# Two queues and half-matrix loads at the head of a fused linear-ReLU-residual kernel

## The chip, the cores and the metric

The kernel runs on one core of a Trainium2 chip. The metric is the device time of one execution in microseconds (us); the median of several runs is compared. A profile is one further execution recorded by the hardware profiler; the stretch it shows, from the first to the last recorded instruction, is called the span.

## The reference

`x` is 4 x 1024 x 512 float32, `cond_512` 4 x 256, `W` 1536 x 512, `b` 512. The batch of 4 is called rows below.

```
hidden = concatenate([cond, cond], -1)                 # 4 x 512
x_mean = mean(x, axis=1, keepdims=True)
fused  = concatenate([x, x_mean, hidden], -1)          # the last two repeated along L
out    = x + relu(fused @ W + b)
```

So W has three parts of 512 rows. The first multiplies x and is the large product. The second multiplies the mean of a row, the third the condition; with b they give one vector for each row, which is added to all 1024 lines of it.

## The kernel before

**Tiles.** x is cut into 32 tiles of 128 lines (eight for each row). For a tile the product needs x turned, with the 512 features on the partitions: four pieces (j = 0 to 3) of 128 x 128. W's first part lies in SBUF as `w_x`, 128 partitions x 4 x 512: partition p holds rows 4p to 4p + 3, and j picks one of the four.

**Precision by splitting.** A float32 value v is split into hi, its value rounded to float32r, and lo = v - hi. A product of one j is three matmuls of 128x512: hi x w_hi, hi x w_lo, lo x w_hi. A tile takes 12 of them, accumulated in one PSUM bank (`po`). The splits of W are `w_hi` (ScalarE, L361) and `w_lo` (VectorE, L363), those of x `hi` (ScalarE, L417) and `lo` (VectorE or GpSimd, L433).

**Turning x.** The first units (tile 0; tile 1; tiles 2 and 3; tiles 4 and 5) are turned by TensorE with an identity matrix (L390), from tiles of x as loaded. All others are turned by VectorE (L392) from a second load of x, called `z`, in pieces of 512 bytes.

**The bias of a row.** Sums of x come from the splitting (L417's accumulator, or L426). `acc` adds the mean's and the condition's parts (L491, L494, L497), is split (`acc_hi`, `acc_lo`, L512 and L516), and a matmul with a matrix of 1/L sums it over the partitions and copies it to all of them (`pb`, L522).

**The end of a tile.** Bias added, ReLU, x added, stored, by VectorE, ScalarE, GpSimd and SP in shares that are written out in sets.

**What sets the order.** A planner, `Plan`, holds for each step its engine's cost, what it depends on and a due time, replays them on a model of the engines, tries 1500 variations of the due times, and keeps the best. Each engine then carries out its steps strictly in that order. What comes before the plan begins is told to it by hand: `plan.done[key]` is when a load of the head is taken to land, `plan.free["sp"]` when the load queue is taken to be free. Of the loads of the head, all are issued by SP, in the order of the table in the code:

```python
for key, at, load in (
    (("x", 0, 0), 4.5, lambda: load_x(0, 0, 1)),
    (("w", 0), 5.7, lambda: load_w(0)),
    ...
    (("x", 0, 1), 8.25, lambda: load_x(0, 1, 1)),
    ...
    (("x", 0, 2), 10.2, lambda: load_x(0, 2, 2)),
    (("x", 1, 0), 11.6, lambda: load_x(1, 0, 2)),
):
```

Behind them SP issues the first quarter of W's second part (`w_mean`), its third part (`w_cond`) and the z pieces. A load is issued when the load eight places before it has landed.

**The head of each engine.** VectorE clears a tile `warm`; TensorE multiplies it nine times (`N_WARM`, L236), turns tile 0, turns the condition (`fill`, L399), multiplies `warm` four times more (`N_FILL`, L403), and then begins with the products ("part" for tiles 0 and 1, one matmul at a time; "product" for later tiles). ScalarE loads its table (L231), issues the load of `cond` (`c_sb`, L240), and splits. `FIRST` is the time from which due times are counted.

Of the kernel before, what the change touches and what calls it, by code (L numbers as in the profile page):

```python
# [11 lines left out]
BF16 = mybir.dt.bfloat16  # L12
AF = mybir.ActivationFunctionType
# [140 lines left out]
def kernel(  # L154
# [22 lines left out]
    nc = tc.nc  # L177
    B, L, D = x.shape
    H = cond.shape[1]
    P = 128  # L180
# [6 lines left out]
    G = 4  # L187
    S_BUFS = 15
    O_BANKS = 5
    N_FIRST = 1  # L190
# [1 line left out]
    Z_BUFS = 3  # L192
    X_BUFS = 4
    O_BUFS = 12
    FIRST = 6.8
    NEVER = 1000.0
    TURN_PE = (0, 1, 2, 3)
    ALONE = 28
# [1 line left out]
    KEEP = (0, 1, 2, 3, 4, 8, 9, 10, 16, 17)  # L200
    LO_POOL = {(r, u, j) for r in (1, 2) for u in (0, 1) for j in (1, 3)} | {(0, 4, 3)}

    N_FILL = 4

    const = ctx.enter_context(tc.tile_pool(name="const", bufs=1))
    xpool = ctx.enter_context(tc.tile_pool(name="xpool", bufs=X_BUFS))
# [10 lines left out]
    plan = Plan(["pe", "dve", "act", "pool", "sp", "aq"])  # L217
    nc_of = {"pe": nc.tensor, "dve": nc.vector, "act": nc.scalar, "pool": nc.gpsimd}

    xv = x.rearrange("r (k p) d -> r p k d", p=P)  # L220
    ov = out.rearrange("r (k p) d -> r p k d", p=P)
    zv = x.rearrange("r (n t) (i d) -> r i t n d", t=Q, i=NQ)
    Wv = W.rearrange("(s p j) o -> s p j o", p=P, j=J)


    warm = const.tile([P, 512], BF16, name="warm")
    nc.vector.memset(warm, 0.0)
    ones = const.tile([P, 1], F32, name="ones")
    nc.vector.memset(ones, 1.0)
    table_warm = const.tile([P, 1], F32, name="table_warm")  # L230
# [6 lines left out]
            pw[:, KH * B :], lhsT=warm[:, :P], rhs=warm[:, KH * B :], start=True, stop=True  # L237
        )
    c_sb = const.tile([B, H], F32, name="c_sb")
    nc.scalar.dma_start(out=c_sb, in_=cond)  # L240
    b_sb = const.tile([P, D], F32, name="b_sb")
    nc.gpsimd.memset(b_sb, 0.0)
    mean32 = const.tile([P, P], F32, name="mean32")
# [21 lines left out]
    xs, zs = {}, {}  # L265
    w_x = xpool.tile([P, J, D], F32, tag="x", name="w_x")
    w_mean = const.tile([P, J, D], F32, name="w_mean")

    def load_x(g, i=0, n=G):
        r, k = divmod(g * G, NK)  # L270
        if not i:
            xs[g] = xpool.tile([P, G, D], F32, tag="x", name=f"x{g}")
        nc.sync.dma_start(out=xs[g][:, i : i + n], in_=xv[r, :, k + i : k + i + n, :])  # L273

    def x_tile(t):
        return xs[t // G][:, t % G, :]
# [4 lines left out]
    def load_z(eng, u, i):  # L281
        r, k0, n = units[u]
        if u not in zs:
            zs[u] = zpool.tile([P, G * NQ, P], F32, tag="z", name=f"z{u}")
        i = (0, 2, 1, 3)[i]
        eng.dma_start(  # L286
            out=zs[u][i * Q : (i + 1) * Q, : n * NQ],
            in_=zv[r, i, :, k0 * NQ : (k0 + n) * NQ, :],
        )

    SP = 0.72
    SPZ2 = 1.85
    SPZ = 1.3
    def load_w(j):
        nc.sync.dma_start(out=w_x[:, j, :], in_=Wv[0, :, j])  # L295

    for key, at, load in (
        (("x", 0, 0), 4.5, lambda: load_x(0, 0, 1)),
        (("w", 0), 5.7, lambda: load_w(0)),
        (("w", 1), 6.9, lambda: load_w(1)),  # L300
        (("w", 2), 7.6, lambda: load_w(2)),
        (("x", 0, 1), 8.25, lambda: load_x(0, 1, 1)),
        (("w", 3), 8.9, lambda: load_w(3)),
        (("x", 0, 2), 10.2, lambda: load_x(0, 2, 2)),
        (("x", 1, 0), 11.6, lambda: load_x(1, 0, 2)),
    ):
        load()
        plan.done[key] = (at - plan.HANDOVER, 0.0, "sp")
    w_cond = xpool.tile([P, 2, KH, D], F32, tag="x", name="w_cond")

    def load_cond():
        nc.sync.dma_start(  # L312
            out=w_cond, in_=W[2 * D : 3 * D].rearrange("(s h p) o -> p s h o", p=P, h=KH)
        )
# [3 lines left out]
    def load_mean(j, n):  # L318
        nc.sync.dma_start(out=w_mean[:, j : j + n, :], in_=Wv[1, :, j : j + n])

    load_mean(0, N_FIRST) if N_FIRST else None
    plan.free["sp"] = 9.4 + SP * N_FIRST
    plan.add("cond", {"sp": 4 * SP}, [], 13, lambda e: load_cond(), later=2.5)
    plan.add("w_mean", {"sp": (J - N_FIRST) * SP}, ["cond"], 14,
             lambda e: load_mean(N_FIRST, J - N_FIRST), later=2.5)
# [1 line left out]
    for n, u in enumerate(by_z):  # L327
        c0 = piece_of[u, 0]
        for i in range(NQ):
# [10 lines left out]
            elif n or i:  # L340
                deps.append(("z", u, i - 1) if i else ("z", by_z[n - 1], NQ - 1 if n > N_BOTH else NQ - 2))
            plan.add(("z", u, i), {"sp": SPZ * units[u][2] / G}, deps, NEVER,
                     lambda e, u=u, i=i: load_z(nc.sync, u, i), later=3.0)
    plan.add(("x", 1), {"sp": 2 * SP}, [], NEVER, lambda e: load_x(1, 2, 2), later=3.0)
    x_order = ["w", 0, 1, "cond"] + list(range(2, B * NK // G))
    for n, g in list(enumerate(x_order))[4:]:
        was = x_order[n - X_BUFS] if n >= X_BUFS else None
        deps = ([] if was is None else [("w_lo", j) for j in range(J)] if was == "w" else
                [("add_cond", k) for k in range(KH)] if was == "cond" else
                [("finished", was * G + i) for i in range(G)])  # L350
        if n > 4:
            deps.append(("x", x_order[n - 1]))
        plan.add(("x", g), {"sp": 4 * SP}, deps, NEVER,
                 lambda e, g=g: load_x(g), later=3.0)


    w_hi = const.tile([P, J, D], F32R, name="w_hi")
    w_lo = const.tile([P, J, D], F32R, name="w_lo")
    for j in range(J):
        plan.add(("w_hi", j), {"act": 0.62}, [("w", j)], NEVER,  # L360
                 lambda e, j=j: nc.scalar.activation(w_hi[:, j, :], w_x[:, j, :], AF.Copy))  # L361
        plan.add(("w_lo", j), {"dve": 0.69}, [("w_hi", j)], NEVER,
                 lambda e, j=j: nc_of[e].tensor_tensor(  # L363
                     w_lo[:, j, :], w_x[:, j, :], w_hi[:, j, :].bitcast(F32), ALU.subtract))
# [14 lines left out]
    def turn(c):  # L379
        u, js = pieces[c]  # L380
        n = units[u][2]
        if c in by_pool:
            v = xT[c] = small.tile([P, G * P], F32, tag="xT", name=f"xT{c}")
        else:
            v = xT[c] = ps_x.tile([P, G * P], F32, tag="x", name=f"xT{c}")
        if u in TURN_PE:
            for i in range(n):
                x_t = x_tile(last_tile[u] - n + 1 + i).rearrange("p (a j) -> p j a", j=J)
                for m, j in enumerate(js):
                    nc.tensor.transpose(v[:, (m * n + i) * P : (m * n + i + 1) * P], x_t[:, j], ident)  # L390
        else:
            nc.vector.transpose(  # L392
                v[:, : n * P].rearrange("p (n t) -> p n t", t=Q),
                zs[u].rearrange("p n (a j) -> p n j a", j=J)[:, : n * NQ, js[0], :],
            )

    def fill():
        for h in range(KH):
            nc.tensor.transpose(  # L399
                pw[:, h * B : (h + 1) * B], c_sb[:, h * P : (h + 1) * P], ident[:B, :B]  # L400
            )
        for _ in range(N_FILL):
            nc.tensor.matmul(  # L403
                pw[:, KH * B :], lhsT=warm[:, :P], rhs=warm[:, KH * B :], start=True, stop=True
            )

    plan.add(("b",), {"act": 0.25}, [("w_hi", J - 1)], FIRST + 4, lambda e: nc.scalar.dma_start(
        out=b_sb[0:1, :], in_=b.rearrange("(o d) -> o d", o=1)), later=3.0)
    plan.add(("fill",), {"pe": 0.22 * N_FILL + 0.2}, [("turn", 0)], 5.8, lambda e: fill())

    def split_hi(c):
        u, js = pieces[c]
# [24 lines left out]
    for c, (u, js) in enumerate(pieces):  # L437
        r, k0, n = units[u]
# [9 lines left out]
        if r == 1 and c == first_piece[1]:  # L448
            deps.append(("term", 0, KH + J - 1))
        w = n * len(js)  # L450
        plan.add(("turn", c), {"pe": 0.12 * w} if u in TURN_PE else {"dve": 0.14 + 0.24 * w}, deps,
                 FIRST + 1.3 * c - 1.0 if u in TURN_PE else NEVER,
                 lambda e, c=c: turn(c))
# [19 lines left out]
    def turn_cond():  # L473
        nc.vector.tensor_scalar(bL, b_sb, float(L), None, ALU.mult)
        nc.vector.tensor_scalar(
            cT, pw[:, : KH * B].rearrange("p (h b) -> p h b", h=KH), float(L), None, ALU.mult
        )

    def add_cond(eng, k):
        eng.tensor_tensor(wc[:, k], w_cond[:, 0, k], w_cond[:, 1, k], ALU.add)  # L480
# [48 lines left out]

    plan.add(("turn_cond",), {"dve": 0.3}, [("fill",), ("b",)], FIRST + 5, lambda e: turn_cond())  # L530
    for k in range(KH):
        plan.add(("add_cond", k), {"pool": 1.33}, ["cond"], NEVER,
                 lambda e, k=k: add_cond(nc_of[e], k))
    n_term = 0
    for r in range(B):
# [3 lines left out]
        for n in range(KH + J):  # L539
            if n < KH:  # L540
                deps = [("add_cond", n), ("turn_cond",)]
                if n_term >= 3:
                    deps.append(before[0])
                plan.add(("weigh", r, n), {"act": 0.72}, deps, NEVER,
                         lambda e, r=r, n=n: weigh(r, n))
                plan.add(("term", r, n), {"pool": 1.33}, done + [("weigh", r, n)], NEVER,
                         lambda e, r=r, n=n: add_term(r, n))
                before = (before if n_term else [])[-2:] + [("term", r, n)]
                n_term += 1
            else:  # L550
                deps = [("total", r), "w_mean"]
                if n == KH:
                    plan.add(("acc", r), {"act": 0.61 if r else 0.73},
                             done + [("bias", r - 1)] if r else deps, NEVER,
                             lambda e, r=r: begin_acc(r))
                    cond_done, done = done, [("acc", r)]
                    if not r:
                        continue
                plan.add(("term", r, n), {"dve": 0.76}, done + deps, NEVER,
                         lambda e, r=r, j=n - KH: mean_term(r, j))  # L560
            done = [("term", r, n)]
        if not r:
# [4 lines left out]
                 lambda e, r=r: acc_split_lo(r))  # L567
        plan.add(("bias_product", r), {"pe": 0.5}, [("acc_lo", r)], NEVER,
                 lambda e, r=r: bias_product(r))
        plan.add(("bias", r), {"act": 0.61}, [("bias_product", r)], NEVER,  # L570
                 lambda e, r=r: bias_copy(r))
# [64 lines left out]
    for t in range(NT):  # L636
        r, k = divmod(t, NK)
        u = unit_of[r, k]
        for h in (0, 1) if t == LAST else (None,):
            key = (t, h) if h else t  # L640
# [7 lines left out]
            for j in range(J):  # L648
                c = piece_of[u, j]
                if t < SINGLY:  # L650
                    for n in range(3):
                        deps = [("lo" if n == 2 else "hi", c), ("w_lo" if n == 1 else "w_hi", j)]
                        plan.add(("part", t, j, n), {"pe": 0.234}, deps, FIRST + 1.4 * j + 0.7 * t + 0.234 * (n + 1),
                                 lambda e, t=t, j=j, n=n: product(t, j, None, (n,)))
# [4 lines left out]
                else:  # L659
# [3 lines left out]
                plan.add(("product", key, j), {"pe": 0.7 if h is None else 0.36},  # L663
                         deps, FIRST + 2.8 * t + (0.7 if h is None else 0.36) * (j + 1) + 1.4 * (h or 0), lambda e, t=t, j=j, h=h: product(t, j, h))
        room = [("stored", t - O_BUFS)] if t >= O_BUFS else []
        if t:
            room.append(("freed", t - 1))
        due = min(FIRST + 2.8 * (t + 9), FIRST + 2.8 * NT - 8)
        if t >= ALONE:
            for h in (0, 1) if t == LAST else (None,):  # L670
                key = (t, h) if h else t
# [52 lines left out]
```

## Time and profile before

| | us |
|---|---|
| median of 3 runs (lowest to highest) | 107.19 (106.97 to 108.67) |
| profiled execution | 107.74 |
| its span | 106.0 |
| TensorE busy with matmuls | 101.3 |
| VectorE busy | 77.5 |
| GpSimd busy | 72.9 |
| ScalarE busy | 59.3 |
| one 128x512 product, issue to result | 0.40 |
| first product starts, from the span's start | 6.91 |
| one 256 KB load of W's first part, issue to landing (median of four) | 5.4 |

PE stands for TensorE's matmuls, PEld for its weight loads, DVE for VectorE, ACT for ScalarE, POOL for GpSimd, SP for SyncE; a q behind a name is the engine's queue, where it issues loads. In a line of the timeline there stand the start, the time taken, the engine, the line of the code, the operation, output<-input, how many, and in brackets how long the engine was idle before and what ended it. A line of the windows gives a stretch, its length, the busy time of PE, PEld, DVE, ACT and POOL with the number of instructions, the granted clock, the DMA engines' mean share and GB/s. Matmuls overlap, so a busy PE is not a PE at its peak.

### The profile page before, as it was taken

The page shows a single profiled execution, that of the slowest core. Times are in us where ns is not written, and L with a number is a line of the kernel's source. Part 1 is how long each engine was busy: PE and PEld are TensorE (multiplying, and loading weights), DVE is VectorE, ACT ScalarE, POOL GpSimd, SP SyncE. Part 2 cuts the span into 40 slices and gives each one's busy share as a digit, 9 for nine tenths or more (in the row PEclk, how much of TensorE's full clock was granted, in tenths as well). Part 3 has the DMA queues.
Part 4 walks back from the last instruction along what each step waited for, and adds up shares of the span by engine and source line. Part 5 has one row for each costly group of instructions (what it writes and reads, how often), then busy time and mean ns, then how long its engine had stood idle before and what let it go on. Part 6 is the DMA issues. An engine that isn't in the chain of part 4 may idle for free.

```text
span 106.0 us, 1470 instructions
## 1 busy us (share of the span) xinstructions
PE 101.3 (96%) x445; PEld 79.1 (75%) x445; DVE 77.5 (73%) x119; ACT 59.3 (56%) x138; POOL 72.9 (69%) x66
## 2 busy tenths in 40 slices
PE   5999999999998999999999999999999999999980
PEld 2456878878886787878888887887887887888870
DVE  1058743296589889999699999997999992097460
ACT  5075356799639967795378878222888340262000
POOL 6000004942796999999999899994999999149400
PEclk9999999999999999999999999999999999999999
DMA  3799999999999999999999999999996995504942
GB/s 71 196 361 398 370 216 209 215 164 205 220 181 189 202 202 237 202 275 262 256 252 343 360 316 197 301 395 394 404 387 212 356 367 220 200 0 162 382 174 74
DMA packets 24193, 26.83 MB, mean 253 GB/s; under 512 B 1269, under 2 KB 14841, under 8 KB 24186
## 3 DMA queue, kind: packets, MB, share of 16 engines
q1 hardware_dynamic: 24176, 26.74, 94.6%
q8 instruction: 3, 0.05, 0.2%
q14 instruction: 4, 0.03, 0.1%
q10 hardware_dynamic: 10, 0.01, 0.0%
HBM read 18.36 MB, written 8.39 MB: 252 GB/s over the span
## 4 chain that ended last, share of the span: by engine, by line
PE 66%; DMA 26%; DVE 3%; SPq 1%; issue 1%; DVEq 0%
PE po_None L596 61%; DMA z<-in_x_dram 20%; DMA w_x<-in_L_cond_W_dram 5%; PE po L596 3%; PE pb L522 2%; DVE xT L392 1%; DVE acc L494 1%; DVE acc_lo L516 1%; DVE o L627 0%; SPq L295 0%; SPq L312 0%; SPq L273 0%; SPq L286 0%; PE po L591 0%; DVEq L392 0%
## 5 line engine op out<-in xcount | busy, mean ns | idle before, releaser
L596 PE MATMUL po_None<-w_hi,hi 128*128 128x512 f32 x124 | 49.8, 402 | 0.0
L596 PE MATMUL po_None<-w_lo,hi 128*128 128x512 f32 x124 | 49.2, 397 | 0.1
L596 PE MATMUL po_None<-w_hi,lo 128*128 128x512 f32 x124 | 49.2, 398 | 0.0
L622 POOL TENSOR_TENSOR o<-o,x 128x512 f32<-128x512 f32 x28 | 35.5, 1301 | 4.2 <-ACT o L619 4.1
L392 DVE STREAM_TRANSPOSE xT<-z 128x512 f32<-128x512 f32 (+1 forms) x28 | 28.5, 1041 | 4.7 <-DMA z<-in_x_dram 3.6
L417 ACT ACTIVATE hi<-xT 128x512 fp32r<-128x512 f32 (+1 forms) x38 | 20.4, 537 | 16.8 <-DVE xT L392 8.5
L596 PEld LDWEIGHTS po_None<-w_hi,hi 128*128 128x128 f32 x124 | 23.4, 189 | 6.3 <-ACT w_hi L361 0.5
L596 PEld LDWEIGHTS po_None<-w_lo,hi 128*128 128x128 f32 x124 | 23.4, 189 | 5.6 <-DVE w_lo L363 0.4
L596 PEld LDWEIGHTS po_None<-w_hi,lo 128*128 128x128 f32 x124 | 23.3, 188 | 5.5
L433 DVE TENSOR_TENSOR lo<-xT,hi 128x512 fp32r<-128x512 f32 (+1 forms) x29 | 16.3, 576 | 8.2 <-ACT hi L417 8.2
L619 ACT ACTIVATE o<-o 128x512 f32<-128x512 f32 x28 | 16.7, 628 | 2.0 <-POOL o L614 1.0
L614 DVE TENSOR_TENSOR o<-po_None,bias 128x512 f32<-128x512 f32 x18 | 11.7, 676 | 6.6 <-issue 4.9
L614 POOL TENSOR_TENSOR o<-o,bias 128x512 f32<-128x512 f32 x10 | 12.9, 1306 | 1.4 <-issue 1.4
L433 POOL TENSOR_TENSOR lo<-xT,hi 128x512 fp32r<-128x512 f32 (+1 forms) x9 | 11.1, 1241 | 2.9 <-ACT hi L417 2.9
L480 POOL TENSOR_TENSOR wc<-w_cond 128x512 f32<-128x512 f32 x2 | 2.5, 1289 | 15.1 <-DMA w_cond<-in_L_cond_W_dram 15.1
L497 DVE SCALAR_TENSOR_TENSOR acc<-w_mean,tot,acc 128x512 f32<-128x512 f32 x15 | 11.3, 755 | 1.5 <-ACT acc L491 1.0
L528 ACT ACTIVATE bias<-pb 128x512 f32<-128x512 f32 x4 | 2.4, 598 | 10.1 <-PE pb L522 10.1
L417 ACT ACTIVATION_READ_ACCUMULATOR hi<-xT 128x1 f32 x36 | 7.0, 194 | 0.0
L508 POOL TENSOR_TENSOR cond<-bL,term 128x512 f32<-128x512 f32 x4 | 5.2, 1297 | 1.8 <-ACT term L503 1.8
L503 ACT ACTIVATE term<-wc,cT 128x512 f32<-128x512 f32 x8 | 5.7, 720 | 1.2 <-POOL cond L508 0.8
L609 ACT ACTIVATE o<-po_None 128x512 f32<-128x512 f32 x10 | 5.7, 590 | 0.8 <-PE po_None L596 0.7
L390 PEld LDWEIGHTS xT<-ident,x 128*128 128x128 f32 x24 | 4.2, 206 | 1.7 <-issue 0.8
(51 smaller groups left out, 58.9 us busy)
## 6 DMA issues: line engine op xcount, KB each, us to landing
out_dram<-o SPq DMA_DIRECT2D x31, 256.0 KB, 5.7
z<-in_x_dram SPq DMA_DIRECT2D x24, 256.0 KB, 9.2
x<-in_x_dram SPq DMA_DIRECT2D x6, 1024.0 KB, 8.2
x<-in_x_dram SPq DMA_DIRECT2D x3, 512.0 KB, 7.8
w_x<-in_L_cond_W_dram SPq DMA_DIRECT2D x4, 256.0 KB, 5.4
w_cond<-in_L_cond_W_dram SPq DMA_DIRECT2D x1, 1024.0 KB, 10.2
w_mean<-in_L_cond_W_dram SPq DMA_DIRECT2D x1, 768.0 KB, 12.4
x<-in_x_dram SPq DMA_DIRECT2D x2, 256.0 KB, 4.2
```

What stands on the lines that cost most here:

```text
L390: nc.tensor.transpose(v[:, (m * n + i) * P : (m * n + i + 1) * P], x_t[:, j], ident)
L392: nc.vector.transpose(v[:, : n * P].rearrange("p (n t) -> p n t", t=Q), zs[u].rearrange("p n (a j) -> p n j a", j=J)[:, : n * NQ, js[0], :],)
L417: nc.scalar.activation(hi[c][:, :m], xT[c][:, :m], AF.Copy, accum_out=sums[:, r, js[0], s : s + 1] if len(js) == 1 else None,)
L433: nc_of[e].tensor_tensor(lo[c][:, :m], xT[c][:, :m], hi[c][:, :m].bitcast(F32), ALU.subtract)
L497: nc.vector.scalar_tensor_tensor(acc[r], w_mean[:, j, :], totals[r][:, j : j + 1], acc[r], ALU.mult, ALU.add)
L503: nc.scalar.activation(terms[r, k], wc[:, k], AF.Copy, scale=cT[:, k, r : r + 1])
L508: nc.gpsimd.tensor_tensor(conds[r], conds[r] if k else bL, terms[r, k], ALU.add)
L596: nc.tensor.matmul(pos[key][:, :w], lhsT=v[p][:, c], rhs=m[:, j, d], start=(not h and todo[key] == 3 * J), stop=(todo[key] == 1),)
L609: nc.scalar.activation(o_tile(t), pos[t], AF.Copy)
L614: nc_of[e].tensor_tensor(v if t >= ALONE else o_tile(t), v, biases[t // NK][:, d], ALU.add)
L619: nc.scalar.activation(outs[t], outs[t], AF.Relu)
L622: nc.gpsimd.tensor_tensor(outs[t], outs[t], x_tile(t), ALU.add)
```

## The change

W's first part is loaded in two halves, two rows (4 KB, contiguous) for each partition. Tile 1 of x and the second half of W are issued by ScalarE, behind `c_sb`. SP then has tile 0, W's first half, tiles 2 and 3, tiles 4 and 5. The table of landings that the planner is told changes with it. `w_hi` may be made by ScalarE or VectorE, as the planner finds; a `w_hi` depends on the half that holds it. `warm` is no tile any more but a constant of 1.0 that the framework sets before the kernel starts, so its memset is gone; one warming matmul fewer stands in `fill`.

```diff
-    FIRST = 6.8
+    FIRST = 6.0
...
-    N_FILL = 4
+    N_FILL = 3
...
-    warm = const.tile([P, 512], BF16, name="warm")
-    nc.vector.memset(warm, 0.0)
+    warm = nc.const_aps.tensor(1.0, [P, 512], BF16)
...
     c_sb = const.tile([B, H], F32, name="c_sb")
-    nc.scalar.dma_start(out=c_sb, in_=cond)
...
-    def load_x(g, i=0, n=G):
+    def load_x(e, g, i=0, n=G):
...
-        nc.sync.dma_start(out=xs[g][:, i : i + n], in_=xv[r, :, k + i : k + i + n, :])
+        e.dma_start(out=xs[g][:, i : i + n], in_=xv[r, :, k + i : k + i + n, :])
...
-    def load_w(j):
-        nc.sync.dma_start(out=w_x[:, j, :], in_=Wv[0, :, j])
-
-    for key, at, load in (
-        (("x", 0, 0), 4.5, lambda: load_x(0, 0, 1)),
-        (("w", 0), 5.7, lambda: load_w(0)),
-        (("w", 1), 6.9, lambda: load_w(1)),
-        (("w", 2), 7.6, lambda: load_w(2)),
-        (("x", 0, 1), 8.25, lambda: load_x(0, 1, 1)),
-        (("w", 3), 8.9, lambda: load_w(3)),
-        (("x", 0, 2), 10.2, lambda: load_x(0, 2, 2)),
-        (("x", 1, 0), 11.6, lambda: load_x(1, 0, 2)),
+    def load_w(e, j):
+        e.dma_start(out=w_x[:, j : j + 2, :], in_=Wv[0, :, j : j + 2])
+
+    nc.scalar.dma_start(out=c_sb, in_=cond)
+    for key, at, e, load in (
+        (("x", 0, 0), 4.4, nc.sync, lambda e: load_x(e, 0, 0, 1)),
+        (("w", 0), 6.4, nc.sync, lambda e: load_w(e, 0)),
+        (("x", 0, 1), 5.9, nc.scalar, lambda e: load_x(e, 0, 1, 1)),
+        (("w", 2), 8.2, nc.scalar, lambda e: load_w(e, 2)),
+        (("x", 0, 2), 8.5, nc.sync, lambda e: load_x(e, 0, 2, 2)),
+        (("x", 1, 0), 9.9, nc.sync, lambda e: load_x(e, 1, 0, 2)),
     ):
-        load()
+        load(e)
...
-    plan.free["sp"] = 9.4 + SP * N_FIRST
+    plan.free["sp"] = 7.8 + SP * N_FIRST
...
-        plan.add(("w_hi", j), {"act": 0.62}, [("w", j)], NEVER,
-                 lambda e, j=j: nc.scalar.activation(w_hi[:, j, :], w_x[:, j, :], AF.Copy))
+        plan.add(("w_hi", j), {"act": 0.62, "dve": 0.45}, [("w", j // 2 * 2)], NEVER, lambda e, j=j: (
+            nc.scalar.activation(w_hi[:, j, :], w_x[:, j, :], AF.Copy) if e == "act" else
+            nc.vector.tensor_copy(w_hi[:, j, :], w_x[:, j, :])))
...
-    plan.add(("fill",), {"pe": 0.22 * N_FILL + 0.2}, [("turn", 0)], 5.8, lambda e: fill())
+    plan.add(("fill",), {"pe": 0.22 * N_FILL + 0.2}, [("turn", 0)], 5.6, lambda e: fill())
```

The planner runs anew with these figures. In the order that it finds, TensorE turns tile 1 before the first product; VectorE makes `w_hi` of j = 0, behind `lo` of tile 0; ScalarE makes j = 1, then `hi` of tile 1, then j = 3, issues the load of b, and makes j = 2. TensorE turns tile 2 after six products. On VectorE the last step of row 0's `acc` stands before the z transposes of the next unit, where one of them stood ahead of it before. On SP the first z piece stands before `w_cond`. Behind the head the same steps are carried out, in part in another order. Lines after the change lie one lower (L595 is L596 of before).

More of the change, by code (lines that the diff above doesn't have):

```diff
@@ L343 @@
                      lambda e, u=u, i=i: load_z(nc.sync, u, i), later=3.0)
-    plan.add(("x", 1), {"sp": 2 * SP}, [], NEVER, lambda e: load_x(1, 2, 2), later=3.0)
+    plan.add(("x", 1), {"sp": 2 * SP}, [], NEVER, lambda e: load_x(nc.sync, 1, 2, 2), later=3.0)
     x_order = ["w", 0, 1, "cond"] + list(range(2, B * NK // G))
@@ L353 @@
         plan.add(("x", g), {"sp": 4 * SP}, deps, NEVER,
-                 lambda e, g=g: load_x(g), later=3.0)
+                 lambda e, g=g: load_x(nc.sync, g), later=3.0)
     w_hi = const.tile([P, J, D], F32R, name="w_hi")
```

## The prediction

> **What bounds the kernel now.** I read the page first (busy shares, chain), then the waits, then the timeline of the first 12 us and the windows of those stretches, and last the timeline around the one late wait.
>
> ```profile
> PE 101.3 (96%) x445; PEld 79.1 (75%) x445; DVE 77.5 (73%) x119; ACT 59.3 (56%) x138; POOL 72.9 (69%) x66
> PE 66%; DMA 26%; DVE 3%; SPq 1%; issue 1%; DVEq 0%
> ```
>
> PE is the bound. The chain has two parts: DMA up to 29.50, then PE to the end. The chain's pieces from 33 us on show PE's pace:
>
> ```profile
> 32.96 0.73 PE pb L522 x2
> ...
> 73.37 18.27 PE po_None L596 x78
> ```
>
> 18.27 / 78 = 0.2342 us for one product. PE's last matmul ends at 102.9. The timeline has the first product here:
>
> ```profile
> 1.19 3.96 PE L236 MATMUL pw<-warm 128*128 128x504 bf16 x9 [1.19 <-DVE ones L229]
> ...
> 5.85 1.02 PE L403 MATMUL pw<-warm 128*128 128x504 bf16 x4
> 6.23 0.62 ACT L361 ACTIVATE w_hi<-w_x 128x512 fp32r<-128x512 f32 x1
> ...
> 6.91 0.50 PE L596 MATMUL po_None<-w_hi,hi 128*128 128x512 f32 x1
> ```
>
> From 6.91 to 102.9 are 95.98 us. Work in it: 372 whole and 24 half products are 384 units, 8 bias products and two half ones (L591) 9 more, 393 x 0.2342 = 92.04. Turning transposes: eight pairs (0.235 each, what the rows from 13.20 to 13.58 leave between two products) and one group of four (0.47) make 2.35; 0.17 is the last result's way out (0.40 taken, 0.234 apart). Sum 94.56, so **about 1.4 us are waits**. From the spacing of ends in the timeline: 0.34 for w_lo at 7.71, 0.19 at 10.56 for the turn of unit 2, 0.14 at 15.32, 0.55 before the bias product at 32.96, 0.11 at 41.25, small rest.
>
> The early waits stem from transfers. Windows of one us each (the last columns are clock, DMA share, GB/s):
>
> ```profile
> 2.00:3.00 1.00, 1.00 (x4) 0.44 (x3) 0.00 (x0) 0.21 (x2) 0.26 (x1) 1.00 0.76 258
> 3.00:4.00 1.00, 1.00 (x4) 0.29 (x2) 0.00 (x0) 0.00 (x0) 0.00 (x0) 1.00 0.91 236
> 4.00:5.00 1.00, 1.00 (x4) 0.43 (x3) 0.00 (x0) 0.00 (x0) 0.00 (x0) 1.00 0.53 121
> 5.00:6.00 1.00, 1.00 (x8) 0.82 (x7) 0.00 (x0) 0.26 (x1) 0.00 (x0) 1.00 0.96 279
> 6.00:7.00 1.00, 0.96 (x5) 0.29 (x3) 0.63 (x2) 0.85 (x2) 0.00 (x0) 1.00 0.99 348
> 7.00:8.00 1.00, 0.93 (x3) 0.57 (x4) 1.00 (x3) 0.91 (x2) 0.00 (x0) 1.00 1.06 408
> ```
>
> Between 2 and 7 us 1.24 MB moved; at the 408 GB/s of the next window it would have been 2.04 MB. So **2.0 us of transfer are lost** while W's first rows load, and in 4 to 5 us the DMA engines are idle half the time though SP had issued nearly all of the head's loads (its issue rows end at 4.87). By the loads' semaphores in the trace, when the last engine reports: x tile 0 lands at 3.32, w0 5.48, w1 7.03, w2 7.70, x tile 1 8.39, w3 9.06, x tiles 2 and 3 10.42, x tiles 4 and 5 11.76.
>
> **The change part by part.**
>
> *Constant for warming.* The memset of warm (0.27) goes; ones comes 0.27 earlier, so PE starts near 0.9 and its nine matmuls (0.42 apart) end at 4.65 instead of 4.94. One fill fewer is 0.255. Worth 0 to 0.55 us in front of the first product, but hidden: the first product waits for W, not for PE. Without that cover it would be those 0.55. ones also releases ScalarE's queue 0.27 sooner.
>
> *DMA issues.* ScalarE issues c_sb (0.55), x tile 1 and W's second half (0.43 each by SP's rows) from about 1.0 to 2.5. Its next work is hi of tile 0, 5.74 before and some 5.35 after, so 2.8 us of idle time hide them; without that they would delay hi by 1.4. SP issues 4 fewer of these, so x tiles 2 and 3 are issued near 1.6 instead of 3.52 and the first z piece now stands before w_cond. The b load (0.23) now sits before the last w_hi on ScalarE; that w_hi is used 2 us later.
>
> *Order on PE.* Tile 1's transposes (0.47) now run before the first product, in time that was waiting: gain 0.47. The first product then needs W's first half whole. VectorE makes w_hi 0 behind lo 0; ScalarE makes w_hi 1 with hi of tile 1 queued behind it. A copy on VectorE isn't in the trace; the rows near it are
>
> ```profile
> 14.43 0.43 DVE L474 TENSOR_SCALAR bL<-b_sb 128x512 f32<-128x512 f32 x1 [1.27 <-DMA b_sb<-in_L_cond_b_dram]
> 6.98 0.68 DVE L363 TENSOR_TENSOR w_lo<-w_x,w_hi 128x512 fp32r<-128x512 f32 x1
> ```
>
> I take 0.43, one source from SBUF like the copy; 0.68 is the other end (+0.25). VectorE then has eleven instructions back to back to 13 us. The order on PE leaves it 0.1 to 0.25 us of waits on them (turns 3 and 5).
>
> *The rest of the order.* The planner runs anew, so later work is placed differently. From 33 us on PE keeps its pace before, with 0.1 us of waits, and nothing there is given more work: I cost it at nothing. If a new order made PE wait once as at 32.96, it would cost 0.5.
>
> *The first product, T.* Earliest, by VectorE: tile 0 turned 4.65 to 5.12, result 0.17, hi 0.60 to 5.93, lo 0.69 to 6.67, w_hi 0.43, with 0.05 a handover 7.15. Otherwise the landing of the first half plus 0.53. After six products comes tile 2's turn, which needs x tiles 2 and 3: at T + 1.41. **This is the new wait:** the order counts on them at 8.5, before they came at 10.42.
>
> Change of the end = (T - 6.91) - 0.47 + (new waits - 1.42).
>
> Best end: first half by 6.6, tiles 2 and 3 by 8.5: T 7.15, waits 0.25: 0.24 - 0.47 - 1.17 = -1.4 us. The bias product's 0.55 goes too: VectorE's acc now stands ahead of the z transposes (0.66 less after z lands), and z lands as much sooner as the head does.
> Worst end of the same order: nothing of the lost 2.0 us comes back. First half 7.7 (when as much had landed as w0 to w2 and x0) to 8.4 (ScalarE's queue takes an equal share, one more 0.26 MB load). T 8.2; turn 2 at 9.64 waits to 10.47, 0.83; 0.16 before product 8 and 0.1: 1.3 - 0.47 - 0.33 = +0.5. With 8.4 the wait at turn 2 shrinks as T grows, the same sum.
> Taken: half of the loss returns, 1.0 us: first half near 7.0, tiles 2 and 3 near 9.3. T 7.5; turn 2 at 8.9 waits 0.4; 0.3 others: 0.6 - 0.47 - 0.72 = **-0.6**. I lean a little to the better side, since two queues give idle engines something to move while W's first pass stalls, and one row of 4 KB needs one such first access instead of two: -0.7.
>
> A rule that speaks against it: the Trainium skill, "DMA: Bandwidth & Descriptors", section "Issuing engines are not separate DMA queues", says loads from several engines run on the same 16 engines and interleave, and save only issue time. By it nothing comes back and the sum is the +0.5 above. The idle half of 4 to 5 us is why I don't follow it whole.
>
> The profiled execution took 107.74, 1.74 around a span of 106.0, and stands 0.55 over the median of 107.19 (106.97 to 108.67). From the median: 107.19 - 0.7 = 106.5.
>
> **Rivals.**
> *Bytes decide (B).* The loss stays, W's half waits for tile 1 and part of the other half. For: the two queues carry the same 2.56 MB, and 350 to 410 GB/s from 6 us on is full. Against: idle engines at 4 to 5. +0.5, time 107.7 (107.3 to 108.3).
> *PE falls back to its slow clock (C), slower than before.* Place: PE has nothing between tile 1's turn (6.45 to 7.0) and T. Warming matmuls took 0.42 up to 4.94 and 0.255 at 5.85: the speed came after 3.75 us of steady work (the windows' clock column says 1.00 all along and doesn't show it). If the hole of 0.7 to 1.3 us keeps PE slow for another such stretch, 3.75 us of work takes twice as long, or 1.9 lost, on B's 0.5: 109.6 (108.7 to 110.5). It decides from a hole long enough to spoil the stretch; the holes before (0.34, 0.3) didn't. The Trainium skill, "TensorE: Matmul & The Clock Gate", Part 1, has the gate watch a free-running window of about 3.4 us; by that a hole of 1.3 leaves it mostly busy, and the loss would be nought.
> *VectorE becomes the bound (D).* With the copy at 0.68 and eleven in a row, waits rise 0.25 to 0.5: 106.9, inside the forecast's range.
>
> **How the numbers follow.** Forecast 0.56 (with D; own range 105.4 to 107.2), B 0.26, C 0.18. Two per cent, about what a measurement of this kernel can tell from no change, is 105.05 to 109.33. The floor of -1.4 is 105.8; below 105.05 needs scatter on top: 0.07. Above 109.33: most of C and little of B, 0.16. The range 105.2 to 109.0 leaves out 0.07 below and 0.13 above.
>
> **What would show it.** Right: L595's first product at 7.3 to 7.7; over 200 GB/s in 4 to 5 us; tile 2's turn waiting under 0.6 on x; bias product of row 0 before 32.5 with a wait under 0.3. Wrong: the first half landing after 7.7, x tiles 2 and 3 after 10 (B); products 0.4 us apart after 7 us (C); PE waiting on w_lo or sum (D).

## The result, and the profile after

The changed kernel takes 110.65 us (median of 6 runs, 109.72 to 111.7), the kernel before 107.56 in the same session (6 runs, 106.84 to 109.48). The ratio is 1.0279, 95% interval 1.0224 to 1.0333: slower, where no difference was forecast. Ratios are of the fast runs alone: a run more than 1.5% above the fastest of its kernel in a session is left out of them. The profiled execution took 109.91 with a span of 108.1; before it was 107.74 with 106.0.

The page, busy time of each engine, and the chain by engine:

```profile
PE 101.5 (94%) x444; PEld 79.4 (73%) x444; DVE 78.2 (72%) x119; ACT 57.6 (53%) x137; POOL 73.0 (68%) x66
PE 81%; DMA 13%; DVE 1%; ACT 1%; ACTq 0%; issue 0%; DVEq 0%
```

TensorE does the same work (101.5 against 101.3) in a span 2.1 us longer, so the question is where it waits. The windows of the head show first that more was moved early, as the change meant:

```profile
2.00:3.00 1.00, 1.00 (x4) 0.43 (x3) 0.00 (x0) 0.22 (x2) 0.27 (x1) 1.00 1.01 305
3.00:4.00 1.00, 1.00 (x4) 0.29 (x2) 0.00 (x0) 0.00 (x0) 0.00 (x0) 1.00 0.94 287
4.00:5.00 1.00, 1.00 (x5) 0.71 (x4) 0.00 (x0) 0.00 (x0) 0.00 (x0) 1.00 0.99 217
5.00:6.00 1.00, 1.00 (x6) 0.58 (x5) 0.00 (x0) 0.40 (x1) 0.00 (x0) 1.00 0.93 311
6.00:7.00 1.00, 0.97 (x5) 0.40 (x4) 0.77 (x2) 0.72 (x2) 0.00 (x0) 1.00 1.05 379
```

From 2 to 7 us 1.50 MB moved (the sum of the last column), against 1.24 before; in 4 to 5 us it is 217 GB/s where it was 121. (How far one trace can be trusted in this is taken up under the rivals below.) By the loads' semaphores tile 0 lands at 3.47, W's first half at 5.73, tile 1 at 6.66, tiles 2 and 3 at 9.23, the second half at 9.70, tiles 4 and 5 at 10.95. The chain in order of time, however, now runs through a load of 2 KB:

```profile
1.93 7.77 DMA w_x<-in_L_cond_W_dram
9.70 0.02 issue
9.72 0.02 ACT w_hi L359
9.74 0.04 issue
9.79 6.42 DMA b_sb<-in_L_cond_b_dram
16.21 0.03 issue
16.24 0.02 DVEq L473
16.26 0.05 issue
16.31 0.43 DVE bL L473
16.73 0.07 DVE cT L474
16.81 0.34 DVE lo L432
17.15 0.05 issue
17.20 0.51 PE xT L389 x2
```

b is issued at 9.79 and lands at 16.21. `bL`, b divided for the mean's matrix, waits for it on VectorE. Behind it in VectorE's order stand `cT` and a `lo`; that `lo` frees the PSUM tile that TensorE's next turn needs; and behind that turn stand all the products. The waits and the timeline show the two engines:

```profile
DVE bL L473 <- DMA b_sb<-in_L_cond_b_dram: 3.2, 1, 3.2
PEld xT L389 <- DVE lo L432: 2.7, 1, 2.7
```

```profile
7.40 0.47 PE L595 MATMUL po_None<-w_hi,hi 128*128 128x512 f32 x1
9.37 0.48 PE L389 MATMUL xT<-ident,x 128*128 128x128 f32 x2 [0.34 <-DMA x<-in_x_dram]
...
14.52 0.39 PE L595 MATMUL po_None<-w_lo,hi 128*128 128x512 f32 x1
16.31 0.43 DVE L473 TENSOR_SCALAR bL<-b_sb 128x512 f32<-128x512 f32 x1 [3.22 <-DMA b_sb<-in_L_cond_b_dram]
17.20 0.51 PE L389 MATMUL xT<-ident,x 128*128 128x128 f32 x2 [2.28 <-DVE lo L432]
```

From the spacing of ends TensorE now waits 0.19 before the first product, 0.58 at tile 2's turn (9.37), 0.41 for `w_hi` of j = 2 (10.93) and **2.55 at 17.20**. Its last matmul ends at 105.04 instead of 102.89, so the 2.55 is more than the whole loss of 2.15.

Where the 2.55 comes from: before, the same place (`bL`, `cT`, `lo`, turn) stood at 15.32 with a wait of 0.14:

```profile
9.23 0.23 ACTq L407 DMA_DIRECT2D b_sb<-in_L_cond_b_dram  x1
14.85 0.74 DVE L433 TENSOR_TENSOR lo<-xT,hi 128x256 fp32r<-128x256 f32 x2
15.32 0.51 PE L390 MATMUL xT<-ident,x 128*128 128x128 f32 x2
```

b now lands 1.87 later (16.21 against 14.34), so the turn comes at 17.20, 1.88 later. And TensorE gets there 0.53 earlier: the new order has 23 products ahead of that turn and the old one 27 (0.94), and tile 1 is turned before the first product (0.47), against a first product that comes 0.49 later and about 0.46 more of waits on the way. 0.14 + 1.88 + 0.53 = 2.55.

### The profile page after: what moved, and what is told of

Read it like the earlier page. It is cut to its first block, busy times and chain, and to the rows that moved or that the text cites. A ratio compares the mean times of both kernels' runs of the same rounds, so it can differ in the third digit from the quotient of the medians.

```text
span 108.1 us, 1466 instructions
## 1 busy us (share of the span) xinstructions
PE 101.5 (94%) x444; PEld 79.4 (73%) x444; DVE 78.2 (72%) x119; ACT 57.6 (53%) x137; POOL 73.0 (68%) x66
## 4 chain that ended last, share of the span: by engine, by line
PE 81%; DMA 13%; DVE 1%; ACT 1%; ACTq 0%; issue 0%; DVEq 0%
PE po_None L595 76%; DMA w_x<-in_L_cond_W_dram 7%; DMA b_sb<-in_L_cond_b_dram 6%; PE po L595 3%; PE pb L521 2%; PE xT L389 1%; ACT L230 1%; DVE bL L473 0%; DVE o L626 0%; ACTq L271 0%; DVE lo L432 0%; PE po L590 0%; DVE cT L474 0%; ACT w_hi L359 0%; DVEq L473 0%
## 5 line engine op out<-in xcount | busy, mean ns | idle before, releaser
L595 PE MATMUL po_None<-w_hi,hi 128*128 128x512 f32 x124 | 49.4, 399 | 0.1
L595 PE MATMUL po_None<-w_hi,lo 128*128 128x512 f32 x124 | 49.4, 399 | 0.0
L595 PE MATMUL po_None<-w_lo,hi 128*128 128x512 f32 x124 | 48.8, 396 | 0.0
L595 PEld LDWEIGHTS po_None<-w_hi,hi 128*128 128x128 f32 x124 | 23.4, 189 | 5.9 <-ACT w_hi L359 0.6
L595 PEld LDWEIGHTS po_None<-w_lo,hi 128*128 128x128 f32 x124 | 23.4, 188 | 5.6
L595 PEld LDWEIGHTS po_None<-w_hi,lo 128*128 128x128 f32 x124 | 23.4, 189 | 5.4
L389 PE MATMUL xT<-ident,x 128*128 128x128 f32 x24 | 5.0, 314 | 2.7 <-DVE lo L432 2.3
```

The lines of the kernel that those rows point to most:

```text
L595: nc.tensor.matmul(pos[key][:, :w], lhsT=v[p][:, c], rhs=m[:, j, d], start=(not h and todo[key] == 3 * J), stop=(todo[key] == 1),)
```

## The experiments

Theory 1: the loss is b's late landing, seen through VectorE's order. Rivals: the loss lies in the new head (a second queue, the new order on TensorE), and b's wait only covers it; or b is late because its queue is slow, whatever else is in flight.

### e1_b_early: b issued ahead of the plan

```diff
+    nc.scalar.dma_start(out=b_sb[0:1, :], in_=b.rearrange("(o d) -> o d", o=1))
     (right behind the loop over the head's loads; the plan's step keeps its place and cost)
-    plan.add(("b",), {"act": 0.25}, [("w_hi", J - 1)], FIRST + 4, lambda e: nc.scalar.dma_start(
-        out=b_sb[0:1, :], in_=b.rearrange("(o d) -> o d", o=1)), later=3.0)
+    plan.add(("b",), {"act": 0.25}, [("w_hi", J - 1)], FIRST + 4, lambda e: None, later=3.0)
```

> The changed kernel with the load of b issued on ScalarE's queue at the head, right behind W's second half; the order of everything else is that of the changed kernel. Theory 1 (the late landing of b, 16.2 us, holds VectorE at bL for 3.2 us, and lo and TensorE's turn behind it for 2.55): the wait before bL vanishes (under 0.3 us), PE's idle time at 17.2 goes, time 110.65 - 2.5 = 108.1, from 107.0 to 108.4. Rival 2 (the two queues' loads are what costs, by the waits of 0.58 at 9.4 and 0.41 at 10.9 and what follows from them): over 109.5. Rival 3 (the clock of PE): time falls by little, granted clock 0.984 in some runs.

Measured: 107.52 (12 runs, 107.35 to 110.37), ratio to the kernel before 1.0017 (0.9978 to 1.0056). The order of everything else is the same, so moving one load of 2 KB brings back the whole loss: theory 1 holds. The timeline shows `bL` without an idle time before it, and a new price:

```profile
5.83 0.25 ACTq L307 DMA_DIRECT2D b_sb<-in_L_cond_b_dram  x1
6.12 0.60 ACT L416 ACTIVATE hi<-xT 128x512 fp32r<-128x512 f32 x1 [3.90 <-DMA w_x<-in_L_cond_W_dram]
7.92 0.47 PE L595 MATMUL po_None<-w_hi,hi 128*128 128x512 f32 x1 [0.53 <-DVE w_hi L361]
13.00 0.42 DVE L473 TENSOR_SCALAR bL<-b_sb 128x512 f32<-128x512 f32 x1
```

b goes out at 5.83 only, 0.08 after W's first half has landed (5.75): a load waits for the load eight places before it, and ScalarE stands still meanwhile, with `hi` of tile 0 behind. The first product comes 0.52 later than in the changed kernel.

### e2_before_b_early: the same edit in the kernel before

> The kernel before with the load of b issued at the head behind c_sb, all else in its order. Theory 1: VectorE's wait of 1.3 us before bL vanishes, but PE waited only 0.14 us behind it, so 107.56 - 0.15, from 107.1 to 107.6. If the wait had held more than the trace shows: under 107.

Measured: 108.22 (12 runs, ten of them 106.94 to 108.84, two at 201.44 and 255.01 for which nothing here gives a reason), ratio 1.0063 (1.0006 to 1.0119): above the 107.1 to 107.6 that were expected. b is issued at 5.49 and lands at 9.84 instead of 14.34. TensorE's last matmul in the profiled run ends at 102.20 instead of 102.89, but the times show no gain: the early b isn't worth anything by itself; it matters only where the order has it on TensorE's path.

### e4_plan_b_late: the planner told when b lands

The load stays where the change put it. Only the planner's figure for its landing is mended:

```diff
-        out=b_sb[0:1, :], in_=b.rearrange("(o d) -> o d", o=1)), later=3.0)
+        out=b_sb[0:1, :], in_=b.rearrange("(o d) -> o d", o=1)), later=6.5)
```

> The changed kernel, only the planner told that b lands 6.5 us after its issue instead of 3.0; b is loaded where it was. The planner moves bL and cT behind two more lo's on VectorE. Theory 1: bL still waits, to about 16.2, but the lo's of three units come before it, and PE's stall falls from 2.55 to under 1; time from 107.4 to 109.2. Rival 2: over 109.5.

Measured: 107.50 (12 runs, 107.3 to 108.39), ratio 1.0025 (0.9988 to 1.0062). b is as late as ever (16.08), but VectorE now makes four `lo` of 128x256 ahead of `bL`, where the changed kernel had two, and `bL` follows without idle time. (The order differs in other places too: VectorE makes a second `w_hi`, at 9.92.)

```profile
13.59 0.42 DVE L432 TENSOR_TENSOR lo<-xT,hi 128x256 fp32r<-128x256 f32 x1
14.48 0.42 DVE L432 TENSOR_TENSOR lo<-xT,hi 128x256 fp32r<-128x256 f32 x1 [0.47 <-ACT hi L416]
15.67 0.42 DVE L432 TENSOR_TENSOR lo<-xT,hi 128x256 fp32r<-128x256 f32 x1 [0.76 <-ACT hi L416]
16.18 0.43 DVE L473 TENSOR_SCALAR bL<-b_sb 128x512 f32<-128x512 f32 x1
```

So the late landing alone costs nothing either. The loss needs both: b late, and an order built on its landing 3.0 us after its issue.

### e8_no_w_cond: why b is late

```diff
-        nc.sync.dma_start(
-            out=w_cond, in_=W[2 * D : 3 * D].rearrange("(s h p) o -> p s h o", p=P, h=KH)
-        )
+        nc.gpsimd.memset(w_cond, 0.0)
```

W's third part is not loaded, so the condition's part is left out of the result.

> The changed kernel without the 1 MB load of W's third part (GpSimd sets w_cond to 0, so the condition's part is left out); b is loaded where it was, at 9.8 us on ScalarE's queue. Theory 1a (a small load waits for all that was issued before it on either queue): with 1 MB less issued ahead, some 2.5 us at 400 GB/s, b lands near 13.7 instead of 16.2, and PE's stall behind bL falls from 2.55 to under 0.5. Rival 1b (a single-row load takes some 6 us by itself): b lands near 16 again.

Measured: 107.72 (one run). b is issued at 9.97 and lands at 13.96, 4.0 us instead of 6.4. TensorE's wait at the turn behind it falls from 2.55 to 0.13, the wait at `bL` from 3.2 to this:

```profile
DVE bL L471 <- DMA b_sb<-in_L_cond_b_dram: 0.8, 1, 0.8
```

So some 2 of the 6 us (6.4 in the changed kernel, 6.1 in e4) were due to a load on the other queue that was issued before b; what the other 4.0 are is not shown. On the whole b takes longer the later it is issued, with a scatter of over 1 us: 3.0 to 4.3 us at 1.80 (e3, e5, e9, e10, e12), 4.3 at 5.49 (e2), 4.1 at 5.83 (e1), 5.1 at 9.23 (before), 6.1 and 6.4 at 9.99 and 9.79 (e4, after). It does not wait for all that was issued before it: in the changed kernel `w_cond` (issued 5.75, landed 16.69) and the z pieces of 9.25 and 9.71 (18.32, 18.64) landed after it.

### e3_one_queue: does the second queue matter?

e1 with tile 1 and W's second half issued by SP, in the order of the table (first half, tile 1, second half, tiles 2 and 3):

```diff
-        (("x", 0, 1), 5.9, nc.scalar, lambda e: load_x(e, 0, 1, 1)),
-        (("w", 2), 8.2, nc.scalar, lambda e: load_w(e, 2)),
+        (("x", 0, 1), 5.9, nc.sync, lambda e: load_x(e, 0, 1, 1)),
+        (("w", 2), 8.2, nc.sync, lambda e: load_w(e, 2)),
```

> As e1_b_early, but tile 1 and W's second half are issued by SP, in the order of the table (tile 0, first half, tile 1, second half, tiles 2 and 3, tiles 4 and 5). Theory 1, with the queues indifferent: within 0.4 us of e1_b_early; first half lands near 5.7, tile 1 near 6.7, second half near 8.1, tiles 2 and 3 near 9.5 (more in order, so w_hi 2 earlier and tile 2 later). Rival 2: 0.5 us or more faster than e1_b_early.

Measured: 108.38 (6 runs), ratio 1.0100 (1.0032 to 1.0169), some 0.9 above e1, where at most 0.4 was expected. Tiles 2 and 3 now land at 10.01, behind the second half (8.66), while the planner still counts on them at 8.5: TensorE waits 1.13 at tile 2's turn and 1.62 at tile 1's. This run changed two things at once, the queue and the order of landing; e9 parts them.

### e5_b_first: b at the very front

e1 with the line for b moved right behind the load of `c_sb`, ahead of tile 1.

> As e1_b_early, but b's load stands right behind c_sb on ScalarE's queue, ahead of tile 1. In e1 the issue had to wait for W's first half (issued at 5.83 us) and hi of tile 0 stood behind it, so the first product came at 7.92 instead of 7.40. Theory 1: b is issued near 1.5 and lands near 5, the first product is back at 7.4, the wait for b is gone: 0.5 us less than e1_b_early, so 107.0 (106.7 to 107.4). Rival: tile 1 and the second half land later by b's issue (0.4) and the first product and w_hi 2 with them: as e1, 107.5.

Measured: **115.23** (6 runs, 114.78 to 115.68), ratio 1.0721 (1.0668 to 1.0773). A plain miss: 107.0 was expected. With the extra load, tile 1's load on ScalarE stands eight places behind W's first half (both report on the same semaphore), so that it waited for that half, and then landed behind much of what SP had issued meanwhile: a quarter of `w_mean` at 11.10 and a z piece at 13.65, but not `w_cond`, issued at 3.78 and landed at 17.08.

```profile
5.80 0.36 ACTq L271 DMA_DIRECT2D x<-in_x_dram  x1
13.87 1.13 PE L390 MATMUL xT<-ident,x 128*128 128x128 f32 x4 [8.01 <-DMA x<-in_x_dram]
14.65 0.78 PE L595 MATMUL po_None<-w_hi,hi 128*128 128x512 f32 x1
15.22 0.63 PE L595 MATMUL po_None<-w_hi,lo 128*128 128x512 f32 x1
```

It is b's case again on a load of 256 KB: issued 4 us later, it lands 7 us later (13.82 against 6.66).

### e6_plan_measured: e5 with the planner told later landings

The table's landings became 5.95, 6.85, 9.9, 9.4, 11.15, b 6.0, and the load queue free at 9.0.

> e5_b_first with the planner told what was measured: first half 5.95, tile 1 6.85, second half 9.9, tiles 2 and 3 9.4, tiles 4 and 5 11.15, b 6.0, load queue free at 9.0. It orders anew: the first product stands ahead of tile 1's turn, VectorE makes w_hi 0 ahead of lo 0. Theory 1: PE's waits after the first product fall below 1 us, the first product starts near 6.7, and the time is 106.2 (105.6 to 107.0), under the kernel before. Rival (PE is bound by its work from the first half's landing on, any order is as good): as e5.

Measured: 114.81 (6 runs), ratio 1.0683 (1.0621 to 1.0746). It missed the 106.2 expected for e5's reason: tile 1 is issued at 6.21 and lands at 14.01. No order hides 8 us at the head.

### e9_one_queue_order: one queue, the landing order of two

e5 with all loads of x and W on SP, in the order in which they land in the changed kernel: tile 0, first half, tile 1, tiles 2 and 3, second half, tiles 4 and 5. b stays on ScalarE behind `c_sb`.

```diff
-        (("x", 0, 1), 5.9, nc.scalar, lambda e: load_x(e, 0, 1, 1)),
-        (("w", 2), 8.2, nc.scalar, lambda e: load_w(e, 2)),
+        (("x", 0, 1), 5.9, nc.sync, lambda e: load_x(e, 0, 1, 1)),
         (("x", 0, 2), 8.5, nc.sync, lambda e: load_x(e, 0, 2, 2)),
+        (("w", 2), 8.2, nc.sync, lambda e: load_w(e, 2)),
```

> As e5_b_first, but SP issues tile 1 and W's second half too, in the order in which they land with two queues: tile 0, first half, tile 1, tiles 2 and 3, second half, tiles 4 and 5. If the second queue matters only by the order of the loads: within 0.4 us of e5_b_first, tiles 2 and 3 at 8.7, second half at 10.0. If the second queue itself brings the loads in sooner: 0.5 us or more slower than e5_b_first, with every landing later by that.

Measured: 107.47 (12 runs, 107.13 to 107.74), ratio 1.0011 (0.9981 to 1.0042): the same as e1 with its two queues (1.0017). The order of issue counts: e3, with one queue too, is at 1.0100. For the second queue the equal times don't decide, since e1 and e9 differ in b's place as well: e1 pays 0.52 at its first product for it (7.92), and e9's first product is as late because tile 1 lands at 7.28 instead of 6.60:

```profile
7.33 0.75 PE L390 MATMUL xT<-ident,x 128*128 128x128 f32 x4 [0.37 <-DMA x<-in_x_dram]
7.83 0.48 PE L595 MATMUL po_None<-w_hi,hi 128*128 128x512 f32 x1
```

The landings of all traces say more. On two queues (after, e1, e4, e8) the first half lands at 5.73 to 6.06 and tile 1 at 6.60 to 7.00; on one (e3, e9 to e12) at 5.63 to 6.14 and 6.82 to 7.28. If the second queue brings something, it is a few tenths of a us at tile 1, within the scatter. What is left of waiting is on `w_hi` of j = 2 and tile 1, which come later than the planner was told:

```profile
PE po_None L595 <- ACT w_hi L360: 0.5, 1, 0.5
```

### e10_one_queue_told: e9 with the measured landings

```diff
-        (("w", 0), 6.4, ...   (("x", 0, 1), 5.9, ...   (("x", 0, 2), 8.5, ...   (("w", 2), 8.2, ...   (("x", 1, 0), 9.9, ...
+        (("w", 0), 6.1, ...   (("x", 0, 1), 7.4, ...   (("x", 0, 2), 8.8, ...   (("w", 2), 10.0, ...  (("x", 1, 0), 12.2, ...
-    plan.free["sp"] = 7.8 + SP * N_FIRST
+    plan.done[("b",)] = (6.0, 0.0, "sp")
+    plan.free["sp"] = 10.4 + SP * N_FIRST
```

The plan's step for b goes.

> e9_one_queue_order with the planner told what e9 measured (first half 6.1, tile 1 7.4, tiles 2 and 3 8.8, second half 10.0, tiles 4 and 5 12.2, b 6.0, queue free at 10.4). In its order two products stand ahead of tile 1's turn. Theory: e9's PE waits of 0.64 (tile 1) and 0.75 (w_hi 2) shrink to under 0.6 together, time 106.6 (106.0 to 107.2), under the kernel before. Rival (the head's loads set when PE has all it needs, whatever the order): 107.2 to 107.6 as e9.

Measured: **106.47** (12 runs, 106.33 to 112.41), ratio 0.9931 (0.9877 to 0.9985): the lowest of these times, and 0.7% under the kernel before, with an interval that ends just below 1. The planner now puts two products ahead of tile 1's turn, where e9's order had TensorE stand still for tile 1:

```profile
6.77 0.50 PE L595 MATMUL po_None<-w_hi,hi 128*128 128x512 f32 x1 [0.23 <-ACT w_hi L361]
7.10 0.40 PE L595 MATMUL po_None<-w_hi,lo 128*128 128x512 f32 x1
7.34 0.63 PE L391 MATMUL xT<-ident,x 128*128 128x128 f32 x4
7.91 0.50 PE L595 MATMUL po_None<-w_lo,hi 128*128 128x512 f32 x1
```

Behind the first product TensorE's early waits come to 0.25, and its last matmul ends at 101.57. The loads of the head are those of e9; e12 below, which has e9's order and ran in the same session, took 107.29, so some 0.8 us come from figures told to the planner. In the two profiled runs the first half also landed at different times, 5.63 here and 6.04 in e9, with the same loads ahead of it.

### e11_second_half_first: e10 with the second half ahead of tiles 2 and 3

The planner is told the landings of e3 (6.1, 7.2, 8.8, 10.2, 11.5), and the load queue free at 9.6.

> As e10, with W's second half issued ahead of tiles 2 and 3 (the order of e3_one_queue) and the planner told e3's landings (6.1, 7.2, 8.8, 10.2, 11.5). e3 lost 1.1 us at the turn of tile 2, which its order had at 8.5; here the planner puts 11 products ahead of that turn. Theory: that wait goes, 106.6 (106.0 to 107.2), like e10. Rival: as e3_one_queue, 108.

Measured: 106.81 (12 runs, 106.41 to 109.27), ratio 0.9976 (0.9930 to 1.0023). With the landings told rightly, the order of these two loads costs 0.3 (106.81 against 106.47) at most, with intervals that overlap; in e3, told wrongly, it cost 0.9.

### e12_warm_tile: e9 with a cleared tile for warming

> e9_one_queue_order with warming by the cleared tile instead of the constant: VectorE's memset (0.27) is back, TensorE begins 0.3 us later. If the constant is worth nothing behind the wait for W, as forecast: within 0.2 us of e9, 107.5. If the earlier start brings the full clock sooner: 0.3 us or more slower.

Measured: 107.29 (12 runs, 107.05 to 107.92), ratio 1.0006 (0.9969 to 1.0042), e9 without the edit 1.0011. The constant is worth nothing that can be told.

## Why the prediction was wrong, point by point

**The step that failed** is the sentence "The b load (0.23) now sits before the last w_hi on ScalarE; that w_hi is used 2 us later". It prices the issue of b and names who stands behind the issue. It doesn't ask when b lands, nor who waits for that. The profile of before held both answers: b took 5.1 us to land there (9.23 to 14.34), and `bL` already stood 1.27 us idle for it; the line with that 1.27 was even shown, as a price row for a copy on VectorE. That idle time cost TensorE 0.14, and I read the 0.14 as a small wait at 15.32 without following it back through `lo` to b. With b followed, the question would have been what cover `bL` has in the new order. Four products fewer ahead of the turn were in the order to be seen. With the old 5.1 us from issue to landing, the wait at 17.20 would have been 0.14 + 0.53 + 0.56 (the later issue) = 1.23; the other 1.31 is the longer landing, 6.4 us against 5.1. The term of the sum that failed is "new waits": taken 0.4 + 0.3, measured 0.58 + 0.41 + 2.55 = 3.54. With the measured terms the sum of the prediction comes out: (7.40 - 6.91) - 0.47 + (3.54 - 1.42) = 2.14, where the last matmul came 2.15 later.

**"The rest of the order ... I cost it at nothing"** looked from 33 us on only. The order also changed between 13 and 17 us.

**The head's terms were near, the first product's by luck.** It was forecast at 7.5 from W's first half landing near 7.0, and came at 7.40 with that half landed at 5.73. What set it was the turn of tile 1, at 6.71 behind tile 1's landing at 6.66, and a wait of 0.19 for VectorE's `w_hi`. Tile 2's wait taken 0.4, measured 0.58; the others taken 0.3, measured 0.41 and the 0.19 in front of T. Tiles 2 and 3 were to land near 9.3, measured 9.23. Take the 2.55 out and the last matmul would end at 105.04 - 2.55 = 102.49, 0.4 before the old one, where the sum had 0.6. e1 has 102.48, but from a first product 0.52 later, so that agreement is in part chance. The last 0.1 of the forecast leaned on a row of 4 KB needing one first access instead of two; no run shows such an access, only how halves and quarters landed (see B below).

**The expected gain isn't in the times, though.** e1, e4 and e9 have no hole of that kind and stand at 1.0011 to 1.0025, with intervals that reach to a gain of 0.1 to 0.2% only. The profiled execution of before (107.74) lies above most medians of its runs (107.19, 107.41, 107.56, 107.59, one 108.09), which eats a good part of the 0.4. And the wait of 0.55 before the bias product of row 0, the largest that the sum gave back, is gone in e2 as well (that product starts at 32.49 instead of 32.96), which has the old loads; whether by b or by chance isn't shown. So 106.5 was about 1.0 too low even with b mended (e1 107.52, e4 107.50).

**The bias product** of row 0 no longer waits, as forecast (two `pb` matmuls back to back behind 57 products in the chain); it runs at 34.79 instead of before 32.5, moved by the hole of 2.55.

```profile
21.44 13.35 PE po_None L595 x57
34.79 0.46 PE pb L521 x2
```

**The rivals.** B's sign of being right, a first half that lands after 7.7, didn't come (5.73). The Trainium skill, "DMA: Bandwidth & Descriptors", section "Issuing engines are not separate DMA queues", says that a second issuing engine saves only issue time. That isn't contradicted: the landings on one queue (first half 5.63 to 6.14) and on two (5.73 to 6.06) overlap, as said under e9. The shape of the loads does more: from 2 to 7 us 1.21 and 1.24 MB moved with quarters (e2, before), 1.31 to 1.41 with halves on one queue, 1.39 to 1.50 on two. But of the 1.3 us that W's first rows seemed to gain (7.03 to 5.73), most may be scatter of one trace: in e2, with the old loads, they are whole at 6.09. C was not what happened in the profiled run: products after 7 us are 0.234 apart and the clock is 1.00. It can't be dismissed for all runs: three of the changed kernel's six have a granted clock of 0.984 and take 111.1 to 111.7, three have 0.998 to 1.000 and take 109.7 to 110.2. These 1.4 us between the groups would account for a median that loses 3.1 where the profiled run loses 2.2. An estimate: in e5 6.83 us at half clock make a mean of 0.970, so 0.984 would be some 3.5 us at half clock, 1.7 us of work. Whether the hole of 2.55 brings the lower clock wasn't shown; e1 and e10, without the hole, show 0.983 and 0.984 in two of 12 runs each, and the kernel before 0.984 in one of 29 (111.41), so it isn't the hole alone. D fell: VectorE's copy took 0.42 as priced, and the 0.19 in front of the first product is all that TensorE waited at the head for VectorE's work; the hole is VectorE standing idle, not busy.

**Two slips of the working** change nothing in the forecast: the chance above 109.0 is given as 0.13 and that above 109.33 as 0.16, though the first can't be the smaller, and ten loads of 256 KB are 2.62 MB, not 2.56.

## What to carry to other kernels

When a change moves a load, price its landing and not its issue: read in the trace how long that load took under the same backlog, then follow its first reader's queue, instruction by instruction, to the engine that bounds. An idle time of an engine off the path (here 1.27 us on VectorE, 0.14 on TensorE) is a wait whose cover is nearly used up, and belongs in the list of what the change may uncover. Where a planner sets the order, a wrong landing in its table can cost more than the late load: about 2.7 us for b (1.0279 to 1.0025), some 0.8 us for the head (e9 or e12 to e10), both mended without touching a transfer. And one trace of the loads of the head isn't enough to count tenths of a us by: the same loads landed up to 0.9 us apart in two executions (W's first rows, before and e2).

## What the runs showed of the hardware that was not expected

- **A small load is held up by the other queue's backlog, though it passes part of it.** b's 2 KB took 3.0 to 6.4 us, on a queue that carried next to nothing else at that time; leaving out 1 MB on SP's queue brought it from 6.4 down to 4.0 (e8, one run). In the changed kernel its first byte moved at 14.58, 4.8 us after issue. The Trainium skill, "DMA: Bandwidth & Descriptors", section "Queues, rings and completion order", says that each DMA engine takes turns between the queues it has work for, packet by packet. By that b should pass the backlog, and in part it does: in e2 it landed at 9.84, ahead of loads that SP had issued 1.5 and 2 us before it (10.52, 11.88). Why it still waited 4.8 us for its first byte isn't shown.
- **One load more at the front can delay a load that stands later,** through the eight places: e5's tile 1, issued at 5.80 instead of 1.51, left TensorE idle for 8 us (5.86 to 13.87).
- **TensorE's clock falls in a long idle stretch.** In e5, with no matmul from 5.86 to 13.87, the windows show the granted clock (before the last two columns) going to half:

```profile
10.00:11.00 1.00, 0.00 (x0) 0.00 (x0) 0.00 (x0) 0.00 (x0) 0.00 (x0) 0.91 1.01 265
11.00:12.00 1.00, 0.00 (x0) 0.00 (x0) 0.00 (x0) 0.00 (x0) 0.00 (x0) 0.50 1.08 309
14.00:15.00 1.00, 1.00 (x5) 1.00 (x6) 0.00 (x0) 0.00 (x0) 0.00 (x0) 0.50 1.04 391
```

It fell 5.0 us after the last work (5.86 to 10.83) and came back 3.8 us after the first (13.87 to 17.66); products in between stand 0.427 apart instead of 0.234.
